# A four-layer graph network on one core: weight factors made one from another, tied to the norm steps of z, in a new order

## The chip, the cores and the metric

The kernel runs on one core of a Trainium2 chip. A core has TensorE (PE) for matmuls, VectorE (DVE), ScalarE (ACT) and GpSimd (POOL) for element-wise work, and SyncE (SP), which here only issues DMAs. Each engine takes its own instructions in the order in which the program lists them and waits for semaphores of the others. The metric is the device time of one execution in microseconds (us). The kernel before took 2358.99 us in the median of three runs (2358.26 to 2367.0).

## The reference

128 graphs of 64 nodes with 512 features each go through four residual layers. Every layer takes `h = max(layernorm(x), 0)` and adds its result to `x`. All is float32.

```
layer 0:  x += hyperconv(norm(relu(hyperconv(h, W1, b1))), W2, b2) + h   # 512 -> 1024 -> 512
layer 1:  A = exp(lrelu(tanh(s_i + s_j))) * adj;  s = (h w) a
          x += (normalised A) h w
layer 2:  weight = adj * exp(query key^T), normalised;  x += weight value
layer 3:  transition = normalised(adj * exp(lrelu(s_j + s_i)))
          H = sum over k = 0..2 of (transition^k h) Wk[k] + bk[k];  x += relu(H)
```

`Wk` is 3 x 512 x 512. The rows of layer 3's bias `bk` add up to one row that is added to every token's `H` before the relu.

## The kernel before

**Tiling.** Two graphs fill the 128 partitions; four such tiles (512 tokens) are a group, and there are 16 groups. Layers 0 and 1 run over all groups first, group after group; their result goes to DRAM (`xmid`) and comes back for layers 2 and 3, which again run over all groups. Two tiles are multiplied by a weight matrix at a time, with Strassen-like schemes of seven block products in place of eight (`strassen`, `seven`, `chained`).

**Layer 0 and 1 of one group.** `part("m")` makes the graph's matrix M from the adjacency (matmul at L777). For each pair of tiles ("h0"/"h1") the norm of x and the left multiplication by M (L579) come first, then seven products with W1 ("p0"/"p1", L678, 512 wide), whose outcome is `z` (L698, L805). Then come z's norm steps ("z0"/"z1"): statistics on DVE (L549, L550), reciprocal root and offset on POOL (L551, L552, L557), scaling on ACT (L817), and a transposition through ACT (L588), a DMA on SP (L589) and ACT again (L590) into `rT`. Seven products with W2 follow ("q0"/"q1", L678, 256 wide), and one with M ("y0"/"y1", L830). Layer 1 ("s", "t0", "e0", "t1", "e1") makes its softmax with a row sent through DRAM and back (`across`, L716 and L720) into the matrix `bd` (L859), then left-multiplies (L579) and runs seven products with w (L678, 256 wide).

**Layer 3.** Its three weight matrices are used in a scheme of 7 x 7 block products of 128 x 128 (L1107, `product`). The weights that it needs are fixed combinations of blocks of `Wk`: seven factors f for each k. `setup_w3` makes one of these 21 pieces: it loads blocks of `Wk[k]` (L521, 256 KB), subtracts them on POOL (`minus`, L525), derives four more tiles on POOL (`factors`, L529 to L531) and stores seven tiles to DRAM (`fac`, four stores at L535). Layer 3 reads them back for each group (L1099, three buffers). In layer 3, `snapshot` (L1116, ACT) copies the running sum of products out of PSUM, `plus` (L1122, DVE) adds another sum to it, and `emit` adds the bias (L1130) and combines tiles (L1131 to L1134), all on POOL, then adds the relu to x on DVE (L1138) and stores the result (L1142).

**Who sets the order.** The program first writes all operations down as a graph (`Graph.op`) with an engine, a cost, a latency and a priority. `Graph.run` then walks through time with these costs and picks on every engine the ready operation with the lowest priority value; the resulting list is emitted. Priorities grow with the group (PERIOD1, PERIOD2), with the work done within a layer (STRETCH), and are shifted by one constant per part (AT). So a changed constant, cost or dependency changes the order of all later instructions, on all engines. Where the walk sees PE idle for over 1 us and a free PSUM bank, `fill` puts in matmuls of ones (L1174) that nobody reads, for three quarters of that time.

**Where the pieces stand.** The pieces of layer 3's weights are written down after group g's layers, with the priority of group g + 1, two in each of the groups 0 to 10; their first load depends on the first tile of group g having been sent to `xmid`.

Of the kernel before, what the change touches and what calls it, by code (L numbers as in the profile page):

```python
# [14 lines left out]
P = 128  # L15
# [153 lines left out]
def tile_adj_preln_d4(  # L169
# [105 lines left out]
    def quad(b):  # L275
# [4 lines left out]

    STRETCH, PERIOD1, PERIOD2 = (2.11, 6.43, 50.7454, 3.1018), 79.8, 149.671
    AT = {
        "x0": -1800.77, "apart": 162.27, "w1": -1056.46, "b1": -1251.68, "w2": 289.41, "w": 187.29, "c1": -506.79,
        "l0": -1396.61, "c2": -766.47, "l1": 284.95, "c": 412.65, "g0": -1390.19, "g1": -1497.17, "g2": -452.82,
        "g3": -792.81, "g": -606.23, "bq": 154.13, "l3": 115.58, "wg": -1172.65, "wp": 197.31, "beg0": -229.22,
        "beg1": -36.07, "end00": 423.2, "end01": 45.77, "end11": 664.32, "new2": 124.83, "new3": -530.75, "end2":
        -7.16, "end3": 48.79, "load1": -431.08, "load2": 1027.47, "m": 12.29, "h0": 9.53, "p0": 10.98, "z0": -29.14,
        "q0": 15.48, "y0": -518.61, "h1": -26.33, "p1": -22.59, "z1": -30.25, "q1": 4.48, "y1": -2.76, "s": -33.08,
        "t0": -25.67, "e0": -522.9, "t1": -42.32, "e1": -53.88, "hT": 483.54, "sh": -254.95, "lq": 629.92, "pt":
        495.66, "v": 131.94, "pv": 641.64, "s3": 571.4, "tt": 605.01, "a0": 651.96, "b0": -437.14, "a1": 681.39,  # L290
        "ws": 401.1, "load3": 250.29, "bk": 902.76,
    }
# [219 lines left out]

    def setup_w3(f, k, when):


        sub, turn = nc.gpsimd.tensor_sub, ["wpturn"]
        src = lambda i, j: Wk3[k].rearrange("(c p) o -> p c o", p=P)[:, 2 * i:2 * i + 2, j * 2 * P:(j + 1) * 2 * P]

        def load(i, j, when=()):
            b = Buf("wp")  # L520
            dma(256, lambda: nc.sync.dma_start(b.t.rearrange("p (q n) k -> p q (n k)", q=2), src(i, j)), when, [b, *turn])  # L521
            return b

        def minus(y, x_, out):
            pool(1.3, lambda: sub(out.t, y.t, x_.t), [y, x_], [out])  # L525

        def factors(F):
            R = Buf("wp")
            pool(0.8, lambda: sub(R.t[:, 1:3], F.t[:, 1::2], F.t[:, 0:2]), [F], [R, *turn])  # L529
            pool(0.53, lambda: sub(R.t[:, 0], F.t[:, 3], R.t[:, 1]), [F, R], [R])  # L530
            pool(0.53, lambda: sub(R.t[:, 3], F.t[:, 2], R.t[:, 0]), [F, R], [R])  # L531
            to = lambda n: fac[f][n].rearrange("p (r k c) -> p r k c", k=3, c=P)[:, :, k, :]
            for n, d, b, v in ((0, slice(0, 2), F, slice(0, 3, 2)), (0, slice(2, 4), R, slice(0, 2)),
                               (1, slice(1, 2), F, slice(3, 4)), (1, slice(0, 3, 2), R, slice(2, 4))):
                dma(128, lambda n=n, d=d, b=b, v=v: nc.sync.dma_start(to(n)[:, d], b.t[:, v]), [b], [("fac", f, n, k, d.start)])  # L535

        terms = (((0, 0),), ((1, 0),), ((1, 1),), ((0, 0), (0, 1), (1, 1), (1, 0)), ((0, 0), (0, 1)),
                 ((0, 0), (0, 1), (1, 1)), ((0, 1), (1, 1)))[f]
        F = load(*terms[0], when)
        for at in terms[1:]:  # L540
            Y = load(*at)
            minus(Y, F, F)
        factors(F)
# [166 lines left out]
    def across(col, r, lat=2.0):  # L710

        b = Buf("rw")
        d = dram.tile([P, T], F32, name=f"row{len(rows)}")
        key = ("row", len(rows))
        rows.append(d)
        dma(4, lambda: nc.sync.dma_start(d, col()), r, [key], lat=lat)  # L716

        def back():
            for s in HALVES:
                nc.sync.dma_start(b.t[s].rearrange("p c t -> p (c t)"), d[s].rearrange("c t -> (c t)").partition_broadcast(C))  # L720
        dma(128, back, [key], [b], 1.2, lat + 0.8 if lat > 2 else 2.0)
        return b
# [35 lines left out]
    def layer0(g):  # L758
# [29 lines left out]
        for t0 in (0, 2):  # L788
# [22 lines left out]
            for i in range(2):  # L811
                z, rT = zs[i], rTs[i]
                mv, rs = norm_stats(lambda k, z=z: z.t[:, k * D:(k + 1) * D], 2, [(z, 0), (z, 1)])
                nm = offset(mv, rs)
                for j in range(2):
                    half = lambda z=z, j=j: z.t[:, j * D:(j + 1) * D]
                    act(0.72, lambda half=half, rs=rs, nm=nm: nc.scalar.activation(half(), half(), AF.Identity, bias=nm.t, scale=rs.t), [(z, j), rs, nm], [(z, j)])  # L817
                    transposed(half, [(z, j)], Buf("tmp"), half, [(z, j)], lambda rT=rT, j=j: rT.t[:, j * KD:(j + 1) * KD, :], [(rT, j)])
                    step(0.1)
# [175 lines left out]
    def layer3(g):  # L995
# [116 lines left out]
        def snapshot(chain):  # L1112
# [4 lines left out]
            return Z  # L1117

        def plus(Z, chain):
            for n, p in enumerate(banks[chain]):  # L1120
# [3 lines left out]
        def emit(i, j, Z):  # L1124


            z = lambda a, b, s=1: Z.t[:, a:b:s]
            add = nc.gpsimd.tensor_add
            cast = lambda n: z(n, n + 1).to_broadcast([P, 2, P])
            pool(0.84, lambda: add(z(0, 4, 3), z(0, 4, 3), bk3_b.t[:, 2 * j * P:2 * (j + 1) * P].rearrange("p (a b) -> p a b", a=2)), [(Z, 0), bk3_b], [(Z, 0)])  # L1130
            pool(0.92, lambda: add(z(1, 3), z(1, 3), cast(0)), [(Z, 0)], [(Z, 0)])  # L1131
            pool(0.92, lambda: add(z(0, 8, 7), z(3, 5), cast(2)), [(Z, 0), (Z, 1)], [(Z, 0), (Z, 1)])
            pool(0.64, lambda: add(z(4, 5), z(7, 8), z(3, 4)), [(Z, 0), (Z, 1)], [(Z, 0), (Z, 1)])
            pool(0.92, lambda: add(z(2, 4), z(5, 7), z(0, 8, 7)), [(Z, 0), (Z, 1)], [(Z, 0), (Z, 1)])  # L1134
            cols = slice(2 * j * P, 2 * (j + 1) * P)
# [9 lines left out]
        product(1, A00, "X", True)  # L1145
        s0 = snapshot("X")
        minus(A11, S2, A00[0], [k[-1] for k in A00[1]])
        product(2, A01, "Y", True)
        plus(s0, "Y")
        emit(0, 0, s0)  # L1150
        product(6, S2, "X", False)
        s1 = snapshot("X")
        minus(A01, S2, A01[0], [k[-1] for k in A01[1]])
        product(5, S1, "X", False)
        s2 = snapshot("X")
        product(3, A01, "X", False)
        s3 = snapshot("X")
        emit(0, 1, s3)
        product(7, A00, "Y", True)
# [35 lines left out]
    for g in range(NG):  # L1195
# [4 lines left out]
        for i, layer in ((0, layer0), (1, layer1)):  # L1200
# [7 lines left out]
            layer(g)  # L1208
        G.prio = (g + 1.0) * PERIOD1
        part("wp")  # L1210
        for i in range(2 * g, min(2 * g + 2, 21)):
            setup_w3(i // 3, i % 3, [("xmid", g, 0)])
    G.prio = NG * PERIOD1
# [9 lines left out]
    for k in range(1, 3):  # L1223
        b = Buf("h")
        dma(256, lambda b=b, k=k: nc.sync.dma_start(b.t, bk3[k].partition_broadcast(P)), [], [b])
        pool(1.3, lambda b=b: nc.gpsimd.tensor_add(bk3_b.t, bk3_b.t, b.t), [b, bk3_b], [bk3_b])
# [69 lines left out]
```

## Time and profile before

| | |
|---|---|
| median of three runs | 2358.99 us |
| profiled execution | 2356.54 us, span 2354.7 us |
| PE busy | 2299.0 us in 14296 matmuls |
| DVE, ACT, POOL busy | 1932.6, 1385.8, 1209.2 us |
| mean DMA rate | 153 GB/s; over 200 GB/s from 1295 us on |
| layers 0 and 1 | from the start to about 1240 us |
| layers 2 and 3 | from about 1210 us to the end |
| pieces of layer 3's weights | loads from 167.7 to 901.6 us |

The span runs from the first to the last instruction. The times of a row in the groups of instructions are the sum over all instructions of that form and the mean of one; the idle time that follows is that of the engine just before them, with the instruction that ended it. A PE instruction's end is modelled, so a wait of PE that is shorter than about 0.16 us does not show as idle time.

### The profile page before, as it was taken

How to read it: one execution, taken by the hardware profiler on the slowest of the kernel's cores; microseconds unless marked ns; L12 is line 12 of the kernel's file. 1: busy time of each engine (PE TensorE's matmuls, PEld its weight loads, DVE VectorE, ACT ScalarE, POOL GpSimd, SP SyncE). 2: the span in 40 equal slices, each digit the busy share in tenths (PEclk: the TensorE clock that was granted, in tenths of full speed). 3: DMA queues.
4: the chain of work that ended last, by engine and by line, in shares of the span. 5: the costliest groups of instructions: out<-in, count | busy, mean ns of one | idle time of the engine just before them, and what ended most of it. 6: DMA issues, size and time to landing. Idle time of an engine off the chain costs nothing.

```text
span 2354.7 us, 39854 instructions
## 1 busy us (share of the span) xinstructions
PE 2299.0 (98%) x14296; PEld 1868.4 (79%) x14296; DVE 1932.6 (82%) x4000; ACT 1385.8 (59%) x1986; POOL 1209.2 (51%) x1777
## 2 busy tenths in 40 slices
PE   9999999999999999999999999999999999999997
PEld 4676667766677666777688899899999999999997
DVE  7968788788888788887867888888888888888886
ACT  4566465765556656576556666565566656566642
POOL 6334565456755566544433555455554545555533
PEclk9999999999999999999999999999999999999999
DMA  8333333333434333232335878777887777787767
GB/s 264 77 75 79 76 92 91 90 71 110 106 94 106 80 93 91 72 81 59 81 77 160 230 217 228 219 210 214 250 228 217 225 214 216 214 249 230 206 199 224
DMA packets 408374, 359.85 MB, mean 153 GB/s; under 512 B 291184, under 2 KB 326768, under 8 KB 408176
## 3 DMA queue, kind: packets, MB, share of 16 engines
q1 hardware_dynamic: 408176, 357.30, 56.1%
q8 instruction: 113, 1.85, 0.3%
q14 instruction: 85, 0.70, 0.1%
HBM read 245.77 MB, written 44.33 MB: 123 GB/s over the span
## 4 chain that ended last, share of the span: by engine, by line
PE 68%; DVE 12%; DMA 10%; ACT 4%; POOL 3%; issue 2%; SPq 1%; POOLq 0%; DVEq 0%; ACTq 0%
PE ps L678 28%; PE ps L1107 18%; PE ps L916 13%; PE ps L579 4%; DMA w2m_wm_a_wf<-fac 3%; PE ps L1053 2%; DMA z_hT<-tmp_mB_xi 2%; DVE rT_vu_tt L1022 2%; PE ps L985 2%; PE ps L830 1%; DMA rw<-row 1%; DVE st L549 1%; DMA h<-o 1%; POOL rs L552 1%; ACT tmp_mB_xi L588 1%
## 5 line engine op out<-in xcount | busy, mean ns | idle before, releaser
L570 ACT ACTIVATE h<-x,nm,rs 128x512 f32<-128x512 f32 x384 | 306.0, 814 | 153.5 <-POOL nm L557 133.3
L551 POOL TENSOR_SCALAR rs<-mv 128x1 f32<-128x1 f32 x320 | 117.1, 366 | 364.5 <-DVE mv L550 345.1
L1107 PE MATMUL ps<-w2m_wm_a_wf 128*128 128x128 f32 x2304 | 298.7, 276 | 2.3 <-DMA w2m_wm_a_wf<-fac 2.2
L1107 PEld LDWEIGHTS ps<-w2m_wm_a_wf 128*128 128x128 f32 x2304 | 280.9, 192 | 8.3 <-DMA w2m_wm_a_wf<-fac 1.9
L678 PE MATMUL ps<-w2m_wm_a_wf,s_s_zz 128*128 128x256 f32 x1152 | 277.3, 380 | 6.3 <-DVE s_s_zz L670 4.0
L1107 PE MATMUL ps<-w2m_wm_a_wf,tmp_mB_xi 128*128 128x128 f32 x2016 | 262.6, 275 | 0.9 <-DMA w2m_wm_a_wf<-fac 0.7
L678 PEld LDWEIGHTS ps<-w2m_wm_a_wf,s_s_zz 128*128 128x128 f32 x1152 | 215.4, 190 | 58.8 <-issue 18.4
L1107 PEld LDWEIGHTS ps<-w2m_wm_a_wf,tmp_mB_xi 128*128 128x128 f32 x2016 | 243.9, 192 | 3.6 <-issue 1.2
L678 PE MATMUL ps<-w2m_wm_a_wf,rT_vu_tt 128*128 128x256 f32 x1024 | 238.8, 380 | 5.7 <-ACT rT_vu_tt L590 5.7
L678 PE MATMUL ps<-wa_mem,mT_sx 128*128 128x512 f32 x512 | 236.1, 593 | 0.7 <-ACT mT_sx L581 0.6
L678 PEld LDWEIGHTS ps<-w2m_wm_a_wf,rT_vu_tt 128*128 128x128 f32 x1024 | 192.2, 190 | 49.7 <-issue 13.9
L552 POOL TENSOR_TENSOR rs<-rs,mhalf 128x1 f32<-128x1 f32 x320 | 209.9, 656 | 26.4
L805 ACT ACTIVATE z_hT<-z_hT 128x512 f32<-128x512 f32 x128 | 80.1, 628 | 208.9 <-DVE z_hT L698 205.4
L549 DVE BATCH_NORM_STATS2 st<-x 128x6 f32<-128x512 f32 x256 | 173.4, 682 | 26.7 <-DMA x<-xm 20.1
L678 PE MATMUL ps<-wa_mem,s_s_zz 128*128 128x512 f32 x384 | 180.1, 595 | 4.5 <-DVE s_s_zz L670 4.1
L678 PEld LDWEIGHTS ps<-wa_mem,mT_sx 128*128 128x128 f32 x512 | 96.3, 190 | 107.1 <-issue 98.8
L706 POOL TENSOR_TENSOR u<-u,row_sh 128x256 f32<-128x256 f32 x96 | 76.2, 804 | 173.0 <-DVE u L648 144.3
L557 POOL TENSOR_SCALAR nm<-mv,rs 128x1 f32<-128x1 f32 x320 | 146.0, 456 | 31.3
L590 ACT COPY rT_vu_tt<-z_hT 128x1024 uint16<-128x1024 uint16 x128 | 146.7, 1158 | 22.9 <-DMA z_hT<-tmp_mB_xi 22.4
L579 PEld LDWEIGHTS ps<-bd,h 128*128 128x128 f32 x1024 | 131.0, 194 | 29.8 <-DVE bd L859 11.8
L968 POOL TENSOR_TENSOR u<-u,wp_bv_bk 128x512 f32<-128x512 f32 x48 | 67.9, 1414 | 153.8 <-ACT u L621 153.8
L588 ACT COPY o<-h 128x1024 uint16<-128x1024 uint16 x128 | 132.2, 1043 | 23.8 <-DVE h L1044 21.3
(191 smaller groups left out, 5116.7 us busy)
## 6 DMA issues: line engine op xcount, KB each, us to landing
w2m_wm_a_wf<-fac SPq DMA_DIRECT2D x112, 768.0 KB, 5.6
w2m_wm_a_wf<-fac SPq DMA_DIRECT2D x112, 576.0 KB, 4.9
x<-xm SPq DMA_DIRECT2D x128, 256.0 KB, 3.9
x<-in_x_dram SPq DMA_DIRECT2D x64, 256.0 KB, 2.8
xm<-x SPq DMA_DIRECT2D x64, 256.0 KB, 2.1
out_dram<-x SPq DMA_DIRECT2D x64, 256.0 KB, 2.8
wp_bv_bk<-in_Wk_dram SPq DMA_DIRECT2D x42, 256.0 KB, 3.0
adj<-in_adj_dram SPq DMA_DIRECT2D x32, 256.0 KB, 4.2
```

Source lines behind the costliest of these rows:

```text
L549: dve(0.69, lambda i=i: nc.vector.bn_stats(st.t[:, i, :], src(i)), [r[i]], [(st, i)])
L551: pool(0.32, lambda: nc.gpsimd.tensor_scalar_add(rs.t, mv.t[:, 1:2], EPS), [mv], [rs])
L552: pool(0.65, lambda: nc.gpsimd.tensor_tensor(rs.t, rs.t, mhalf, ALU.pow), [rs], [rs])
L557: pool(0.47, lambda: nc.gpsimd.tensor_scalar(nm.t, mv.t[:, 0:1], rs.t, -1.0, op0=ALU.mult, op1=ALU.mult), [mv, rs], [nm])
L570: act(0.82, lambda: nc.scalar.activation(h.t, xx.t, AF.Relu, bias=nm.t, scale=rs.t), [xx, nm, rs], [h])
L579: nc.tensor.matmul(quad(p)[:, c, :], h.t[:, c * P:(c + 1) * P], rhs(), start=True, stop=True)
L588: act(1.05, lambda: nc.scalar.copy(u16(planes.t).rearrange("p (q c) -> p q c", q=2), u16(src()).rearrange("p (c q) -> p q c", q=2)), ksrc, ...
L590: act(1.16, lambda: nc.scalar.copy(u16(dst()).rearrange("p c (k q) -> p c k q", q=2), u16(back()).rearrange("p (q c r) -> p c r q", q=2, c ...
L678: nc.tensor.matmul(p.t[:, :n], lhs()[:, c, :], rhs(c), start=first and c == 0, stop=c == kc - 1, skip_group_check=True)
L805: act(0.63, lambda: nc.scalar.activation(z.t[:, cols], z.t[:, cols], AF.Relu), [(z, j)], [(z, j)])
L916: nc.tensor.matmul(pair(p.t)[:, o, :], a, b, start=first and o == 0 and c == 0, stop=c == 1, skip_group_check=True)
L1107: nc.tensor.matmul(inner(p, q)[:, r, :], at()[:, k, :], w_.t[:, r, k, :], start=first and r == 0 and k == 0, stop=k == 2, skip_group_check ...
```

## The change

Five things are changed.

1. `setup_w3`: the factors of each k are now made in the sequence 0, 4, 5, 3, 1, 2, 6, k after k. Factor 0's tile stays in its buffer (`chain3`), and the next three are each made from the last by one subtraction. A k needs 8 loads and 4 subtractions, where it was 14 and 7.
2. The pieces' place: none stands in group 0, two in each of the groups 1 to 10 and one in group 11, with the priority of group g. The loads depend on the end of z's offset (L557) of an earlier half, the POOL work on the end of z's offset of a half of group g.
3. The bias of layer 3 is added by `bias` right after each snapshot, no longer inside `emit`.
4. The last `emit` of the program, that of block (1, 0) of group 15, runs its four adds on DVE.
5. All of STRETCH, PERIOD1, PERIOD2 and AT have new values; `across` is written down with a latency longer by 1.3 us (write) and 0.7 us (read) where layer 3 calls it; `minus` with 1.35 us in place of 1.3; the second and third load of `bk` wait for the first.

```diff
-    STRETCH, PERIOD1, PERIOD2 = (2.11, 6.43, 50.7454, 3.1018), 79.8, 149.671
+    STRETCH, PERIOD1, PERIOD2 = (1.9884, 2.1221, 50.9861, 3.7462), 79.959, 161.557
     AT = {
-        "x0": -1800.77, "apart": 162.27, "w1": -1056.46, "b1": -1251.68, "w2": 289.41, "w": 187.29, "c1": -506.79,
+        "x0": -2165.99, "apart": 359.07, "w1": 560.57, "b1": -128.79, "w2": 2266.0, "w": 629.08, "c1": 83.74, "l0":
...
-    def setup_w3(f, k, when):
+    chain3 = {}
+
+    def setup_w3(n, when, at):
+        k, n = n // 7, n % 7
+        f, blocks = ((0, ((0, 0),)), (4, ((0, 1),)), (5, ((1, 1),)), (3, ((1, 0),)), (1, ((1, 0),)), (2, ((1, 1),)), (6, ((0, 1), (1, 1))))[n]
...
-            pool(1.3, lambda: sub(out.t, y.t, x_.t), [y, x_], [out])
+            pool(1.35, lambda: sub(out.t, y.t, x_.t), [y, x_, *at], [out])
...
-            pool(0.8, lambda: sub(R.t[:, 1:3], F.t[:, 1::2], F.t[:, 0:2]), [F], [R, *turn])
+            pool(0.8, lambda: sub(R.t[:, 1:3], F.t[:, 1::2], F.t[:, 0:2]), [F, *at], [R, *turn])
...
-        terms = (((0, 0),), ((1, 0),), ((1, 1),), ((0, 0), (0, 1), (1, 1), (1, 0)), ((0, 0), (0, 1)),
-                 ((0, 0), (0, 1), (1, 1)), ((0, 1), (1, 1)))[f]
-        F = load(*terms[0], when)
-        for at in terms[1:]:
-            Y = load(*at)
+        got = [load(*b) for b in blocks]
+        F = chain3[k] if 0 < n < 4 else got.pop(0)
+        if n == 0:
+            chain3[k] = F
+        for Y in got:
             minus(Y, F, F)
         factors(F)
...
-        dma(4, lambda: nc.sync.dma_start(d, col()), r, [key], lat=lat)
+        dma(4, lambda: nc.sync.dma_start(d, col()), r, [key], lat=lat + 1.3 if lat > 2 else 2.0)
...
-        dma(128, back, [key], [b], 1.2, lat + 0.8 if lat > 2 else 2.0)
+        dma(128, back, [key], [b], 1.2, lat + 1.5 if lat > 2 else 2.0)
...
                 nm = offset(mv, rs)
+                G.last_write["z", g, k] = G.ops[-1]
...
+        def bias(j, Z):
+            add = nc.gpsimd.tensor_add
+            pool(0.84, lambda: add(Z.t[:, 0:4:3], Z.t[:, 0:4:3], bk3_b.t[:, 2 * j * P:2 * (j + 1) * P].rearrange("p (a b) -> p a b", a=2)), [(Z, 0), bk3_b], [(Z, 0)])
...
-            add = nc.gpsimd.tensor_add
+            last = g == NG - 1 and (i, j) == (1, 0)
+            add, on = (nc.vector.tensor_add, lambda c, *a: dve(c * 0.55, *a)) if last else (nc.gpsimd.tensor_add, pool)
             cast = lambda n: z(n, n + 1).to_broadcast([P, 2, P])
-            pool(0.84, lambda: add(z(0, 4, 3), z(0, 4, 3), bk3_b.t[:, 2 * j * P:2 * (j + 1) * P].rearrange("p (a b) -> p a b", a=2)), [(Z, 0), bk3_b], [(Z, 0)])
-            pool(0.92, lambda: add(z(1, 3), z(1, 3), cast(0)), [(Z, 0)], [(Z, 0)])
...
+            on(0.92, lambda: add(z(1, 3), z(1, 3), cast(0)), [(Z, 0)], [(Z, 0)])
...
         s0 = snapshot("X")
+        bias(0, s0)
...
         s1 = snapshot("X")
+        bias(0, s1)
...
         s2 = snapshot("X")
+        bias(1, s2)
...
-        G.prio = (g + 1.0) * PERIOD1
+        G.prio = g * PERIOD1
         part("wp")
-        for i in range(2 * g, min(2 * g + 2, 21)):
-            setup_w3(i // 3, i % 3, [("xmid", g, 0)])
+        if g:
+            for k in range(2):
+                if 2 * g - 2 + k < 21:
+                    setup_w3(2 * g - 2 + k, [("z", g - 1 + k, 1 - k)], [("z", g, k)])
...
-        dma(256, lambda b=b, k=k: nc.sync.dma_start(b.t, bk3[k].partition_broadcast(P)), [], [b])
+        dma(256, lambda b=b, k=k: nc.sync.dma_start(b.t, bk3[k].partition_broadcast(P)), [bk3_b], [b])
```

## The prediction, made before the changed kernel was run

> **What bounds the kernel now.** First the page's busy times, and PE's row in its 40 slices:
>
> ```profile
> PE 2299.0 (98%) x14296; PEld 1868.4 (79%) x14296; DVE 1932.6 (82%) x4000; ACT 1385.8 (59%) x1986; POOL 1209.2 (51%) x1777
> ...
> PE   9999999999999999999999999999999999999997
> ```
>
> PE sets the time. It idles 55.7 of 2354.7 us, so nothing outside its instructions can gain more than that. Where it idles is asked of the windows (columns: window, its length, busy us of PE, weight loads, DVE, ACT and POOL with instruction counts, PE clock, DMA share, GB/s). I cut them at 152 (the first groups are in), at 943 (the pieces' last work), at 1150 to 1296 (layers change) and at the last groups:
>
> ```profile
> 0.00:152.00 152.00, 141.73 (x549) 86.05 (x549) 121.32 (x246) 84.86 (x119) 64.33 (x100) 0.99 0.52 143
> 152.00:943.00 791.00, 776.48 (x3350) 552.57 (x3351) 648.12 (x1365) 473.24 (x661) 453.76 (x692) 1.00 0.37 91
> 943.00:1150.00 207.00, 206.55 (x901) 150.63 (x900) 163.00 (x358) 125.31 (x177) 101.00 (x161) 1.00 0.28 67
> 1150.00:1296.00 146.00, 143.09 (x849) 118.59 (x849) 107.31 (x240) 93.29 (x133) 47.25 (x89) 1.00 0.46 118
> 1296.00:2290.00 994.00, 978.74 (x8170) 910.34 (x8167) 850.35 (x1721) 592.16 (x875) 516.27 (x703) 1.00 0.79 222
> ```
>
> The reader is to compare the second line with the third. Both are the same layers 0 and 1. With pieces PE idles 14.5 us in 791 (1.84%), without them 0.45 in 207 (0.22%). At the lower rate the 791 us would idle 1.7, so 12.8 us is the most that a better place for the pieces can give. What PE waits for in 152 to 943 (columns: total us, times, longest):
>
> ```profile
> POOL wp_bv_bk L525 <- DMA wp_bv_bk<-in_Wk_dram: 28.7, 8, 8.8
> POOL wp_bv_bk L529 <- DMA wp_bv_bk<-in_Wk_dram: 14.5, 6, 3.5
> PE ps L579 <- DVE bd L859: 6.1, 6, 1.9
> ```
>
> POOL runs in order, and stands up to 8.8 us at a subtraction (L525) whose block has not landed; z's offset and layer 1's work on POOL are queued behind it, and DVE's softmax matrix (`bd`) then reaches PE late. PE's other waits there are 3.8 us for DVE's products' inputs (L670), 3.7 for `rT` from ACT (longest 1.4) and 1.4 for x. In layers 2 and 3 PE waits longest for layer 3's own loads:
>
> ```profile
> PE ps L1107 <- DMA w2m_wm_a_wf<-fac: 7.8, 9, 1.7
> ```
>
> **The Trainium skill.** "Perfetto Trace Analysis", section "Tensor Engine Instruction (MATMUL, LD_WEIGHTS)": the other engines' wait queues feed strictly ordered execution queues, and a matmul's end is estimated. The 8.8 us stand of POOL agrees with the order; for the ends I use start-to-start pitches (0.429 us for a 512-wide matmul of layer 0's W1, 0.216 for 256 wide, 0.112 for 128 wide). "SBUF — State Buffer", section "🔬 SBUF: two separate sides": DVE and GpSimd share a port pair as an exclusive lock. L525 takes 1.26 to 1.77 us for one shape, which agrees but does not prove it. "GPSIMD Engine Reference", section "4.1 Engine selection": a two-input add is about twice as slow on GpSimd; here 0.72 us for 128x256 (L1132) against 0.42 on DVE (L872).
>
> **The change part by part**, summed against the profiled execution's 2356.5 us (the median is 2.45 above it).
>
> *Tail, −0.9.* The end in the timeline:
>
> ```profile
> 2347.57 0.56 DVE L1122 TENSOR_TENSOR s_s_zz<-ps,s_s_zz 128x384 f32<-128x384 f32 x1
> 2348.27 0.72 POOL L1132 TENSOR_TENSOR s_s_zz<-s_s_zz 128x256 f32<-128x256 f32 x1 [0.24 <-DVE s_s_zz L1122]
> 2349.07 0.46 POOL L1133 TENSOR_TENSOR s_s_zz<-s_s_zz 128x128 f32<-128x128 f32 x1
> 2349.60 0.72 POOL L1134 TENSOR_TENSOR s_s_zz<-s_s_zz 128x256 f32<-128x256 f32 x1
> 2350.36 0.76 DVE L1138 SCALAR_TENSOR_TENSOR x<-s_s_zz,x 128x256 f32<-128x256 f32 x2 [2.23 <-POOL s_s_zz L1134]
> ```
>
> From L1122's end (2348.13) to L1138's start POOL needs 2.23. On DVE the three adds cost 0.42 + 0.28 (halved tile, between 0.21 and 0.42) + 0.42 = 1.12, with some 0.1 between them. The gain is 1.0; the preceding block's relu instructions stand ahead of L1131 on DVE, so I take 0.9, range 0 to 1.05. The bias (L1130, 64 of 947 ns) goes to before the last product; the same instruction runs, it only leaves the tail, where it was already over at 2347.2.
>
> *Pieces in 152 to 943, −9.8.* 18 loads of 256 KB and 9 subtractions fewer: 9 × 1.37 = 12.3 us of POOL and 18 × about 0.4 of SP's issue, none of it on PE's path by itself. What counts is the waits behind them. A piece's loads now start a half earlier than its work, so POOL no longer stands at L525 (28.7) or L529 (14.5). Ties to z's offset put the 2.9 us of piece work after the offset that z needs. And the order gives more cover: counting the matmuls listed between producer and user, z's norm to its first W2 product had 6 products of 1.72 + 0.86 + 1.72 + 0.9 = about 13.8 us ahead of it, and has one M product (0.86) and one left multiplication (0.89) more, 15.5. The softmax matrix had 23.0 to 25.6 and gets 27.3. Waits of at most 1.4 (`rT`) and 1.9 (`bd`) against 1.75 and about 2.6 more cover are gone: 3.7 + 6.1. The 3.8 of L670 and the 1.4 for x I leave. Bounds: −12.8 as above, or 0 if these waits had another source: two of the longest go back to a late softmax row and a late transposition, no piece.
>
> *New tight places, +1.* In the changed order a copy of layer 1's second half on ACT (L646, 0.37 us) must end within one product of 0.86 us, where it had at least 1.7. ACT waits for PE there now, not PE for ACT. Range 0 to +5.
>
> *Head, −1.* Five fill matmuls more (32 to 37 before the layers settle) at 0.223 cost 1.1; PE's longest wait there, 2.9 us for the first W2 product, sits in the old order. Range −3.5 to +3.
>
> *Change of layers, +4.8.* The fills (columns: start, duration, then what ran, how often; two instructions make one matmul):
>
> ```profile
> 1195.21 3.73 PE L1174 MATMUL ps<-ones 128*128 128x128 f32 x32
> 1200.07 1.99 PE L678 MATMUL ps<-w2m_wm_a_wf,rT_vu_tt 128*128 128x256 f32 x8 [1.13 <-ACT rT_vu_tt L590]
> ```
>
> 32 instructions are 16 fill matmuls at 0.223. PE still waits 1.13 after them: the fills cover a real wait. Between the layers there were 37 such matmuls, and will be 55: 18 × 0.223 = 4.0, with 0.8 of wait left after them (they fill three quarters of the time that the order foresees as idle). Fills cannot be skipped, so this is paid even if the data come earlier. Other side: fewer idle holes elsewhere in that stretch return up to 4.8, range 0 to +6.
>
> *Layers 2 and 3, 0.* The loads from `fac` stand in nearly the same sequence on SP, with the same 5.99 us of products between the buffer's release and its use; only the place of layer 2's products among them differs. Range −2 to +4. Longer latencies of `across` and the wait among the `bk` loads issue nothing new; they only shift the order, which is already counted; hidden by 100s of us of cover before layer 3.
>
> Sum: −0.9 − 9.8 + 1 − 1 + 4.8 + 0 = −5.9, so 2350.6 for a profiled execution, and 2353.0 on the median's scale.
>
> **Rivals.** *A, the pieces were all of it.* Idle time falls to the rate of the stretch without pieces: −12.8, head −3.5, tail −0.9, change of layers 0: 2359.0 − 17.2 = 2341.8. For it: the third window line. Against it: 18 more fills that must run, and the two waits above that come from no piece.
>
> *B, ACT becomes the bound of layer 1 (slower).* The new order is the same in twelve groups, so one tight place is paid twelve times. If an activation of z (about 1.05 us with its neighbour's 0.59 copy) stands ahead of L646, PE is late by 1.5 us per group: +18 in place of the +1 and of part of the gain, 2359.0 + 12 = 2371. It decides once ACT is over 0.3 us late at that copy, twice per group. Against it: ACT is 60% busy and waits for PE at L646 28 times, 19.9 us in the whole span.
>
> *C, nothing arrives.* The waits have another source, the row through DRAM (42.3 us of DVE's waits, which PE mostly does not see) or the transposition (3.1 us, as long with pieces' DMAs beside it as without); gains and fills cancel: 2359 + 4.8 − 0.9 − 1 = 2362.
>
> *D, a new wait in place of the old one.* The stores of a piece wait for POOL on SP's queue, and z's transposition (L589) is issued behind them. A piece takes 2.9 us of POOL after the offset, z's scaling and first transposition about 1.9 on ACT; SP then is 1.0 late, within the 1.75 of added cover. It costs from 0.75 us more on, then about 1 per piece: 21 in place of nothing, 2353 + 21 = 2374.
>
> **How the numbers follow.** A measurement of this kernel can tell about 0.5%, 11.8 us. The forecast as summed, with its own range of 2346 to 2360, has 0.45; C 0.10; A 0.25; B and D together 0.20. A lies below 2347.2 and most of B and D above 2370.8. Part of the forecast's low end adds 0.03 to faster, and the ends of C and of a bad change of layers 0.02 to slower: faster 0.28, within 0.5% 0.50, slower 0.22. Leaving out a tenth on each side gives 2338 to 2370.
>
> **What would show it.** POOL's waits at L525 and L529 for DMA under 10 us in place of 43.2; PE's wait at L579 for `bd` under 2 us; no `rT` wait over 0.5 in groups 2 to 11; idle PE in 152 to 943 near 5 us. 226 fill instructions in place of 180, and PE idle at the change of layers about as before. The tail from last matmul to end 6.3 us in place of 7.2. B shows as PE's wait at L678 for ACT's L646 or DVE's L670, alike in each group; D as SP standing at L535 ahead of L589. The prediction is wrong if a wait repeats in every group, or if layers 2 and 3 move by over 4 us though their order hardly changes.

## The result and the profile after

The changed kernel took 2351.77 us in the median of 14 runs (2345.95 to 2356.56), the kernel before beside it 2358.7 (2356.51 to 2367.0). The ratio is 0.9965, with a 95% interval of 0.9954 to 0.9976: about 8 us, or 0.35%, which is less than 0.5%. It was measured once more beside some of the experiments below: 0.9968 (0.9956 to 0.9979). The profiled execution has a span of 2345.6 us, where that of before had 2354.7.

The page of the changed kernel, busy times and PE's row in its 40 slices:

```profile
PE 2301.3 (98%) x14342; PEld 1876.8 (80%) x14342; DVE 1936.0 (83%) x4004; ACT 1386.6 (59%) x1986; POOL 1201.9 (51%) x1764
...
PE   9999999999999999999999999999999999999998
```

PE has 46 instructions more, the 23 matmuls of ones that were foreseen, and idles 44.3 us in place of 55.7. The windows of the changed kernel (window, length, busy us of PE, weight loads, DVE, ACT, POOL, clock, DMA share, GB/s):

```profile
0.00:152.00 152.00, 141.62 (x546) 85.49 (x547) 124.38 (x252) 87.59 (x122) 73.42 (x113) 0.99 0.51 149
152.00:943.00 791.00, 787.53 (x3423) 566.52 (x3422) 637.23 (x1380) 478.82 (x671) 445.24 (x675) 1.00 0.35 85
943.00:1150.00 207.00, 205.55 (x891) 147.93 (x890) 162.64 (x351) 129.92 (x178) 103.87 (x166) 1.00 0.30 71
1150.00:1296.00 146.00, 142.05 (x908) 122.91 (x907) 108.70 (x237) 86.89 (x128) 51.34 (x90) 1.00 0.44 116
1296.00:2290.00 994.00, 978.71 (x8146) 909.72 (x8145) 866.26 (x1720) 590.08 (x869) 509.85 (x697) 1.00 0.81 222
```

In 152 to 943, PE's idle time has gone from 14.5 to 3.5 us; in each of the other windows it has moved by about 1 us at most. All that PE waited for in that window (total us, times, longest):

```profile
PE ps L583 <- DVE bd L864: 3.8, 5, 2.1
PE ps L835 <- DVE y_qT L712: 1.0, 1, 1.0
PE ps L583 <- ACT h L574: 0.6, 1, 0.6
```

Lines are four to thirteen higher in the changed kernel (L579 is L583 now, L859 is L864, L670 is L674, L1174 is L1187). The waits for `rT`, for the products' sums on DVE (L670) and for x are gone, and `bd` is down from 6.1 to 3.8, of which 2.1 stand at 151.4 us, before a group is steady. POOL's waits for pieces, 43.2 us in 14 stands before, are gone too: its only wait for that buffer and a DMA is now one for the bias rows, L1241.

A window that is fixed in time holds other work in each kernel. A table at equal work is better. Its marks are the starts of the last product with M of layer 0 (L830) in groups 2 and 12, of layer 2's last product (L985) in group 2 and of layer 3's last product in group 15, found in each trace by counting PE's instructions in the program's order. The second column is safe, since both orders repeat from group to group there, and PE runs the same 3120 instructions in it besides fills; the columns beside it carry a constant, since the marks stand a little differently among the other work in each order.

| profiled execution (us) | start to layer 0, group 2 | to group 12 | to layer 2, group 2 | to the last product | to the end |
|---|---|---|---|---|---|
| before | 267.4 | 737.9 | 378.8 | 962.6 | 8.0 |
| changed | 268.4 | 723.9 | 382.1 | 964.4 | 6.9 |
| changed, measured again | 266.1 | 722.8 | 380.9 | 966.1 | 6.9 |

The gain is in ten steady groups of layers 0 and 1, 14 to 15 us, or 1.4 per group. The change of layers gives back 2 to 3, the tail gives 1.1. Layers 2 and 3 took 962.6 to 968.4 us in all traces of this study with nearly the same order, so their 2 to 3.5 us here are scatter. The second column scatters less: in six traces that have the changed order there (these two and the four of the fill matmuls below) it lies between 722.8 and 724.0.

Not all of the 14 us is idle time of PE. In the second column, first before, then changed:

```profile
267.39:1005.32 737.93, 724.76 (x3128) 515.19 (x3126) 608.45 (x1274) 446.30 (x624) 424.13 (x640) 1.00 0.36 90
268.36:992.23 723.87, 720.54 (x3122) 516.54 (x3121) 586.10 (x1271) 444.04 (x621) 409.26 (x621) 1.00 0.36 85
```

Idle time falls from 13.2 to 3.3 us, by 9.8. The other 4.2 us is in PE's busy time: 0.7 for three fill matmuls that only the old order has there (3 × 0.223), the rest in the same matmuls. The clock is no rival for the gain: neither trace has a stretch at half clock between these marks.

The tail in the timeline of the changed kernel, on DVE now:

```profile
2339.54 0.56 DVE L1131 TENSOR_TENSOR s_s_zz<-ps,s_s_zz 128x384 f32<-128x384 f32 x1 [0.32 <-PE ps L1112]
2340.14 0.42 DVE L1141 TENSOR_TENSOR s_s_zz<-s_s_zz 128x256 f32<-128x256 f32 x1
2340.60 0.29 DVE L1142 TENSOR_TENSOR s_s_zz<-s_s_zz 128x128 f32<-128x128 f32 x1
2340.92 0.43 DVE L1143 TENSOR_TENSOR s_s_zz<-s_s_zz 128x256 f32<-128x256 f32 x1
2341.38 0.76 DVE L1147 SCALAR_TENSOR_TENSOR x<-s_s_zz,x 128x256 f32<-128x256 f32 x2
```

From the end of the last sum (2340.10) to L1147 it is 1.28 us, where POOL needed 2.23: 0.95 gained. Each add costs what was read from the rows of before (0.42, 0.29, 0.43), and the bias is out of the way.

### The profile page after: what moved, and what is told of

Same layout as the page of the kernel before. It is cut to its first block, busy times and chain, and to the rows that moved or that the text cites. A ratio compares the mean times of both kernels' runs of the same rounds, so it can differ in the third digit from the quotient of the medians.

```text
span 2345.6 us, 39929 instructions
## 1 busy us (share of the span) xinstructions
PE 2301.3 (98%) x14342; PEld 1876.8 (80%) x14342; DVE 1936.0 (83%) x4004; ACT 1386.6 (59%) x1986; POOL 1201.9 (51%) x1764
## 4 chain that ended last, share of the span: by engine, by line
PE 75%; DMA 9%; DVE 9%; ACT 3%; POOL 2%; issue 2%; SPq 0%; DVEq 0%; POOLq 0%; ACTq 0%
PE ps L682 35%; PE ps L921 13%; PE ps L1112 13%; PE ps L583 5%; DMA w2m_wm_a_wf<-fac 4%; PE ps L1058 2%; PE ps L990 2%; DVE o L382 2%; PE ps L835 2%; DMA x<-xm 2%; PE ps L952 1%; DVE st L553 1%; DMA wa_q<-o 1%; PE ps L468 1%; DMA rw<-row 1%
## 5 line engine op out<-in xcount | busy, mean ns | idle before, releaser
L555 POOL TENSOR_SCALAR rs<-mv 128x1 f32<-128x1 f32 x320 | 102.5, 320 | 349.0 <-DVE mv L554 329.6
L561 POOL TENSOR_SCALAR nm<-mv,rs 128x1 f32<-128x1 f32 x320 | 160.9, 504 | 30.4
L583 PEld LDWEIGHTS ps<-bd,h 128*128 128x128 f32 x1024 | 128.7, 194 | 35.0 <-issue 17.1
L822 ACT ACTIVATE z_hT<-z_hT,nm,rs 128x512 f32<-128x512 f32 x128 | 103.8, 813 | 73.3 <-POOL nm L561 73.3
```

The lines of the kernel that those rows point to most:

```text
L555: pool(0.32, lambda: nc.gpsimd.tensor_scalar_add(rs.t, mv.t[:, 1:2], EPS), [mv], [rs])
L561: pool(0.47, lambda: nc.gpsimd.tensor_scalar(nm.t, mv.t[:, 0:1], rs.t, -1.0, op0=ALU.mult, op1=ALU.mult), [mv, rs], [nm])
L583: nc.tensor.matmul(quad(p)[:, c, :], h.t[:, c * P:(c + 1) * P], rhs(), start=True, stop=True)
```

## The experiments

Two explanations of the 14 us have to be told apart. In the *wait theory*, POOL's stands at late blocks of the pieces made PE late, and the pieces' new form ended that. In the *order theory*, the old order of layers 0 and 1 had too little cover whatever the pieces did, and the new constants ended that. Where an edit says that the order is kept, every instruction that stays is issued in the same sequence on its engine.

**Both kernels without the pieces' work, order kept.** The loads and POOL instructions of 20 of the 21 pieces are left out, so layer 3's weights are not made. In both kernels alike, here as in the one before:

```diff
-            dma(256, lambda: nc.sync.dma_start(b.t.rearrange(...), src(i, j)), when, [b, *turn])
+            dma(256, (lambda: nc.sync.dma_start(b.t.rearrange(...), src(i, j))) if first else (lambda: None), when, [b, *turn])
...
-            pool(0.8, lambda: sub(R.t[:, 1:3], F.t[:, 1::2], F.t[:, 0:2]), [F], [R, *turn])
+            pool(0.8, (lambda: None) if not first else lambda: sub(R.t[:, 1:3], F.t[:, 1::2], F.t[:, 0:2]), [F], [R, *turn])
```

> The kernel before in its own order, with the loads and all POOL work of 20 of the 21 pieces left out (their stores stay, so layer 3's weights are wrong). Wait theory (POOL standing at pieces' late blocks makes PE late): PE's idle time in 152 to 943 falls from 14.5 to about 3 us, the kernel is 8 us faster (5 to 12.8). Order theory (too little cover in the old order, whatever the pieces do): bd and rT waits stay, 0 to 3 us faster.

> The changed kernel in its own order, with the loads and all POOL work of 20 of the 21 pieces left out (stores stay, layer 3's weights are wrong). Wait theory: the change has already taken the pieces off PE's path, so at most 1 us faster than the changed kernel, and level with the kernel before without its pieces but for the tail and the change of layers. Order theory: also about 0 to 1 us faster, but then 5 us or more ahead of the kernel before without its pieces in layers 0 and 1. If pieces still cost something here: 2 to 4 us faster.

Measured: 0.9968 (0.9957 to 0.9980) for the kernel before without pieces and 0.9955 (0.9943 to 0.9967) for the changed one, both against the whole kernel before. So all of the pieces together cost the old order 0.32%, 7.5 us, and the new order 0.10 to 0.13% (0.9965 or 0.9968 against 0.9955), 2 to 3 us, which is at the edge of what the intervals tell. At equal work, from group 2 to 12: 729.2 and 718.5 us. In that stretch the pieces cost 8.7 us in the old order (737.9 − 729.2) and 4.3 to 5.4 in the new; without these pieces the new order is still 10.7 us ahead. In the new order four waits of PE for `bd`, of 0.2 to 0.7 us, go with the pieces (441, 585, 658 and 731 us); they are 1.7 of those 4.3 to 5.4. What PE waits for in the old order without pieces, in 152 to 943:

```profile
PE ps L678 <- DVE s_s_zz L670: 3.4, 9, 0.5
PE ps L579 <- DVE bd L859: 2.8, 4, 1.6
PE ps L678 <- DVE x L831: 1.4, 2, 0.7
PE ps L678 <- DVE x L872: 0.8, 3, 0.3
PE ps L678 <- ACT rT_vu_tt L590: 0.4, 1, 0.4
```

Of the old waits for `rT` (3.7) and `bd` (6.1), 3.3 and 3.3 us were the pieces' doing. The others stand there unchanged. They are small and come back from group to group; first the kernel before, then the same without pieces, both in PE's timeline:

```profile
417.75 3.70 PE L678 MATMUL ps<-wa_mem,s_s_zz 128*128 128x512 f32 x8 [0.45 <-DVE s_s_zz L670]
452.57 1.99 PE L678 MATMUL ps<-w2m_wm_a_wf,s_s_zz 128*128 128x256 f32 x8 [0.69 <-DVE x L831]
```

```profile
414.54 3.70 PE L678 MATMUL ps<-wa_mem,s_s_zz 128*128 128x512 f32 x8 [0.38 <-DVE s_s_zz L670]
449.38 1.99 PE L678 MATMUL ps<-w2m_wm_a_wf,s_s_zz 128*128 128x256 f32 x8 [0.70 <-DVE x L831]
```

So both theories hold a part, and the order's part is the larger one in this stretch: 3 to 4 us by the pieces, 10.7 by the order. What the old order had ahead of such a wait for DVE's sum (L670) is read from the timeline of the kernel before without pieces, ACT, DVE and PE:

```profile
485.48 0.81 ACT L570 ACTIVATE h<-x,nm,rs 128x512 f32<-128x512 f32 x1
486.20 0.56 ACT L581 COPY mT_sx<-ps 128x512 f32<-128x512 f32 x1
486.70 0.66 DVE L382 SCALAR_TENSOR_TENSOR o<-h,wa_q 128x512 f32<-128x512 f32 x1
487.28 0.42 DVE L670 TENSOR_TENSOR s_s_zz<-mT_sx 128x256 f32<-128x256 f32 x1
487.76 3.70 PE L678 MATMUL ps<-wa_mem,s_s_zz 128*128 128x512 f32 x8 [0.38 <-DVE s_s_zz L670]
```

The copy `mT` (L581) feeds DVE's sum (L670) and that the next seven W1 products. ACT takes a normalisation of x (L570, 0.81 us) ahead of the copy. But the copy is there at 486.76, and the sum starts 0.5 us later: DVE first takes L382, which reads such a normalised x (`h`). In the new order neither stands ahead, and the sum starts when the copy ends:

```profile
340.40 0.58 ACT L585 COPY mT_sx<-ps 128x512 f32<-128x512 f32 x1
341.01 0.43 DVE L674 TENSOR_TENSOR s_s_zz<-mT_sx 128x256 f32<-128x256 f32 x1 [0.29 <-ACT mT_sx L585]
...
343.15 0.81 ACT L574 ACTIVATE h<-x,nm,rs 128x512 f32<-128x512 f32 x1
```

This is a reading of timelines; no run moved these instructions alone, and it explains one kind of the repeated waits, not all of the 10.7 us.

**The pieces ahead of z's norm, order otherwise kept.** Is the tie to the end of z's norm steps worth anything?

```diff
                 mv, rs = norm_stats(lambda k, z=z: z.t[:, k * D:(k + 1) * D], 2, [(z, 0), (z, 1)])
+                if i == 1:
+                    o = G.ops[-2]
+                    o.fn = lambda o_fn=o.fn, key=(g, k): ([q() for q in early.get(key, [])], o_fn())
                 nm = offset(mv, rs)
...
+        def pool(cost, fn, r, w):
+            early.setdefault(at[0][1:], []).append(fn)
+            return G.op("POOL", cost, lambda: None, r, w)
```

> The changed kernel with each piece's POOL work issued ahead of the reciprocal root and offset of the half's second tile, in place of behind them; all else in the same order. If the tie to the end of z's norm steps matters: rT of the second tile is later by 2.9 us (4.3 with a subtraction), which is beyond the 1.75 us of added cover: about 1.2 us per piece, 24 us slower than the changed kernel (10 to 40). If the cover alone carries it: within 3 us of the changed kernel.

Measured: 1.0058 (1.0044 to 1.0071), so 21 us slower than the changed kernel (1.0058 − 0.9968 = 0.0090). From group 2 to 12 it takes 741.0 us in place of 723.9; an estimated 5.1 of these 17 us (3 × 1.7) are three stretches at half clock, which the last section looks at. But PE does not wait where the prediction had counted the cover, at the W2 products for `rT`. The longest and the `rT` wait of this kernel in 152 to 943 (the two others there are 0.8 and 0.5; its lines are four higher than the changed kernel's; L678 here is the sum on DVE):

```profile
PE ps L686 <- DVE s_s_zz L678: 18.5, 9, 2.8
PE ps L686 <- ACT rT_vu_tt L598: 0.5, 1, 0.5
```

It is the copy `mT` again, now on ACT's side: POOL late, z's four ACT instructions late (3.6 us together), the copy behind them late, DVE's sum late, and then the other half's W1 products. The sizes agreed with the forecast by luck.

**A smaller delay at the same place.** Two reciprocal roots of one element per partition ahead of the second tile's norm steps, in the 21 halves that have a piece:

```diff
+                if i == 1 and 2 <= 2 * g + k < 23:
+                    o = G.ops[-2]
+                    late = lambda: [nc.gpsimd.tensor_tensor(late_t, ones[:, :1], mhalf, ALU.pow) for _ in range(2)]
+                    o.fn = lambda o_fn=o.fn: (late(), o_fn())
```

> The changed kernel with two more reciprocal roots of one element per partition (about 0.67 us each, 1.33 us together) on POOL ahead of the offset of the half's second tile, in the 21 halves that have a piece. Cover theory: 1.33 us is within the added cover of 1.75 us, so within 3 us of the changed kernel, where 2.9 us or more cost 22 us; it also shows that 28 us more of POOL's work cost nothing by themselves. If every delay of z is paid: 21 x 1.33 = 28 us slower; if POOL's amount of work counts (the 12.3 us that the change saves): 12 us or more slower.

Measured: 0.9999 (0.9987 to 1.0012), 7 us slower than the changed kernel, where under 3 was expected of the cover. From group 2 to 12 it takes 728.6 us, 4.7 more. PE's timeline and ACT's and DVE's beside it show the place:

```profile
338.27 1.17 POOL L821 TENSOR_TENSOR late<-ones,mhalf 128x1 f32<-128x1 f32 x2
...
343.45 1.04 ACT L593 COPY tmp_mB_xi<-z_hT 128x1024 uint16<-128x1024 uint16 x1
344.40 0.58 ACT L586 COPY mT_sx<-ps 128x512 f32<-128x512 f32 x1
345.01 0.42 DVE L675 TENSOR_TENSOR s_s_zz<-mT_sx 128x256 f32<-128x256 f32 x1 [1.43 <-ACT mT_sx L586]
345.49 1.13 PE L683 MATMUL ps<-wa_mem,s_s_zz 128*128 128x512 f32 x2 [0.46 <-DVE s_s_zz L675]
```

1.17 us of delay give 0.46 us of wait. The new order's slack at this copy is thus about 0.7 us and not 1.75, and `rT` is not what is late first. The run with the pieces ahead says the same: a piece without a subtraction holds POOL for 1.89 us there (563.33 to 565.22) and gives a wait of 1.10, one with a subtraction 3.23 (338.43 to 341.66) and 2.45. Each time all but 0.7 to 0.8 us arrives at PE. The wait comes back once per group, with 0.45 to 0.65 us from 345 us on. That only so much of POOL's work counts as passes this slack also answers whether POOL's amount matters: 42 × 0.561 = 23.6 us more of it cost 7 us here, 4.8 of them in waits for DVE's sums (L675).

**The pieces and the constants, each alone.** The order is worked out anew in both. First the kernel before with the new `setup_w3`, its place and its ties:

```diff
-        for i in range(2 * g, min(2 * g + 2, 21)):
-            setup_w3(i // 3, i % 3, [("xmid", g, 0)])
+        if g:
+            for k in range(2):
+                if 2 * g - 2 + k < 21:
+                    setup_w3(2 * g - 2 + k, [("z", g - 1 + k, 1 - k)], [("z", g, k)])
```

> The kernel before with the change's setup_w3, its place and its ties alone (parts 1 and 2); constants, tail, bias and across as before, so the order is worked out anew from the old constants. If the pieces' rewrite by itself takes the waits away: PE's idle time in 152 to 943 falls from 14.5 to about 8 us, as without pieces, ratio to the kernel before 0.997 to 0.998. If it helps only with the new constants: 0.999 to 1.002. If the old constants place the new pieces badly: over 1.002.

Measured: 0.9983 (0.9973 to 0.9994), 4 us faster than before, between two of the expected cases. From group 2 to 12: 735.8 us, 2.1 less than before; POOL does not stand at a piece any more, but PE's small waits for DVE's sums stay:

```profile
PE ps L682 <- DVE s_s_zz L674: 4.8, 11, 0.5
PE ps L583 <- DVE bd L864: 2.5, 4, 0.9
PE ps L682 <- ACT rT_vu_tt L594: 1.8, 3, 0.8
```

(From the waits of 200 to 1000 us.) Then the changed kernel with the old `setup_w3` in its old place:

```diff
-        G.prio = g * PERIOD1
+        G.prio = (g + 1.0) * PERIOD1
         part("wp")
...
+        for i in range(2 * g, min(2 * g + 2, 21)):
+            setup_w3(i // 3, i % 3, [("xmid", g, 0)])
```

> The changed kernel with the old setup_w3 and the old place of the pieces (parts 1 and 2 undone); constants, tail, bias and across of the changed kernel, order worked out anew. If the order's cover is a gain of its own and the old pieces cost their 7.5 us on top of it: ratio 0.998 to 0.999. If the new constants' cover also hides the old pieces: 0.996 to 0.997. If the new constants need the new pieces: over 1.001, with fill matmuls and a repeated wait in layers 0 and 1.

Measured: 1.0067 (1.0053 to 1.0081), 16 us slower than before and 23 slower than the changed kernel. The list now has fill matmuls in steady groups, pairs like these in PE's timeline:

```profile
792.17 1.28 PE L1183 MATMUL ps<-ones 128*128 128x128 f32 x10
...
795.78 2.39 PE L1183 MATMUL ps<-ones 128*128 128x128 f32 x20
```

From group 2 to 12 this kernel takes 742.4 us, 18.6 more than the changed one. Of these, 13.9 are in PE's busy time, with 58 fill matmuls there (12.9 us at 0.223) where the changed kernel has none, and 4.7 in its idle time. So the parts cannot be added up. The new constants pay only with the new pieces. The new pieces alone bring half of the gain in time, but only 2.1 of 14 us in layers 0 and 1; the rest of their 4 us lies in layers 2 and 3 (958.4 us to the last product), whose order moved as well.

**Late loads, order otherwise kept.** The 12 loads whose blocks are subtracted are issued when their subtraction comes up:

```diff
-            pool(1.35, lambda: sub(out.t, y.t, x_.t), [y, x_, *at], [out])
+            pool(1.35, lambda: (late.pop(0)(), sub(out.t, y.t, x_.t)), [y, x_, *at], [out])
...
-        got = [load(*b) for b in blocks]
+        late = []
+        got = [load(*b, *([late.append] if 0 < n < 4 or m else [])) for m, b in enumerate(blocks)]
```

> The changed kernel with the 12 loads whose blocks are subtracted issued on SP only when their subtraction comes up on POOL, as late as before; all else in the same order. Wait theory: POOL stands about 2.5 to 3 us at 12 subtractions (some 30 us in all), and what is queued behind them is late for PE: 3 to 8 us slower than the changed kernel. If only work ahead of z's offset hurts, and what is behind the pieces has slack: within 2 us of it.

Measured: 0.9978 (0.9966 to 0.9989), beside 0.9968 for the changed kernel: not told apart. The edit did not bring about what it was made for. SP is far enough ahead of POOL that the blocks were there in most cases:

```profile
POOL wp_bv_bk L529 <- DMA wp_bv_bk<-in_Wk_dram: 4.8, 4, 1.9
```

4.8 us of standing and not 30. Even so, it took 726.0 us from group 2 to 12, outside the 722.8 to 724.0 of the six traces, with three waits of PE for DVE's sums (1.4 us) that the changed kernel does not have; it is one trace. It leaves open what long stands of POOL behind z's norm would cost in the new order.

**The fill matmuls.** The prediction took each matmul of ones for paid. Without those at the change of layers, with as many as before, and with a third more everywhere:

```diff
-        for _ in range(int(gap * FILL / (0.224 if filled else 0.448))):
+        for _ in range(0 if 5 <= len(filled) < 10 else int(gap * FILL / (0.224 if filled else 0.448))):
```

> The changed kernel without the 55 matmuls of ones between 1140 and 1270 us. If they run where PE would not have had to wait, as the prediction priced them: 4 us faster (up to 12.3 if none covers a wait). If they only fill real waits: 0. If PE's clock falls without them: 1 to 5 us slower, with a lower granted clock in 1140 to 1290.

```diff
+        for _ in range({5: 5, 6: 3, 7: 5, 8: 16, 9: 8}.get(len(filled), int(gap * FILL / (0.224 if filled else 0.448)))):
```

> The changed kernel with 37 matmuls of ones at the change of layers (5, 3, 5, 16 and 8) in place of 55, as many as the kernel before has. Priced as in the prediction, 18 x 0.223: 4 us faster than the changed kernel. If they fill real waits and hold the clock, as the run without any of them says: 0 to 3 us slower.

> The changed kernel with 37 matmuls of ones at the change of layers once more; the first time its runs fell in two groups, near 2348 and near 2356 us, and a third more fill matmuls cost nothing. If the 18 fill matmuls matter: again 0.999 to 1.001 and two groups. If the groups are none of the fills' doing: 0.996 to 0.998, as the changed kernel beside the kernel before.

```diff
+        for _ in range(int(gap * FILL * 4 / 3 / (0.224 if filled else 0.448))):
```

> The changed kernel with every run of fill matmuls a third longer (the whole of the foreseen gap in place of three quarters, some 37 matmuls more). If fills hold PE's clock through waits that are real: 0 to 4 us faster. If each is paid, at 0.223 us: 8 us slower. If they fit into waits and the clock does not fall there anyway: within 2 us.

Measured: 1.0003 (0.9992 to 1.0014) with none, 1.0000 (0.9987 to 1.0013) and 0.9996 (0.9985 to 1.0007) with 37, 0.9971 (0.9959 to 0.9983) with a third more. On balance none of them is paid at 0.223 us: a third more cost nothing that can be told, and taking them away makes the kernel 7 to 9 us slower. Without fills, PE waits longer at the same places, for instance here at the change of layers:

```profile
1254.75 5.66 PE L921 MATMUL ps<-z_hT,wa_mem 128*128 128x256 f32 x16 [5.74 <-ACT z_hT L594]
```

and the clock falls there, to half (the columns are those of the windows above; the clock is the third number from the end):

```profile
1252.00:1255.00 3.00, 0.25 (x1) 0.25 (x2) 2.86 (x10) 1.94 (x3) 1.91 (x5) 0.50 0.69 137
1255.00:1258.00 3.00, 3.00 (x8) 2.37 (x9) 1.82 (x6) 2.60 (x3) 1.83 (x2) 0.50 0.00 0
```

In all, the records show 13.7 us of half clock at 1146, 1252 and 1450 us, where the first profile of the changed kernel has none between 155 us and its last product; the profiled execution is 4.8 us longer. The mean granted clock of each run is on record too, and settles it for the run without fills: 0.9944 in the mean of its 14 runs, where the two measurements of the changed kernel have 0.9976 and 0.9971. Over 2350 us that is an estimated 13 us of lost clock in place of 5.5 and 7, so 6 to 8 of the 8 to 9 us. The fills' worth there is that PE's clock does not fall.

With 37 fills it is settled in part only. The two profiled executions are level with the changed kernel up to the mark in layer 2 (382.1 and 380.4 in the third column). But the 14 runs of the second lie between 2347.6 and 2357.3 us and those of the changed kernel on the same chip between 2344.6 and 2350.6, and no trace is of one of the longer runs. Their mean clocks, 0.9964 and 0.9965, account for 1.5 to 3 of the 7 to 8 us; what makes the rest stays open. With a third more, 42 matmuls, the clock was 0.9986, an estimated 3.5 us less lost than in the changed kernel beside it: these fills may cost a little and give it back.

**The changed kernel once more**, as the control for all of these:

> The changed kernel once more, beside the kernel before on the chip of this call. The 22 us of the early pieces, the 8 us of the two roots and the 8 us of the 18 fill matmuls were all taken against a ratio of 0.9965 from elsewhere. If that holds here: 0.9954 to 0.9976. If this chip gives the change less: 0.998 to 1.000, and those three costs shrink by as much.

Measured: 0.9968 (0.9956 to 0.9979), as the first time. It ran beside the late loads and the third more fills. The other experiments ran where only the kernel before stood beside them, so their distance to the changed kernel goes through the two ratios. Nothing that computes the whole result came out faster than it; the version with a third more fills is the same within the interval.

## Why the prediction was right, and where its steps failed

The time, 2353.0 forecast against 2351.77, and the case, faster by under 0.5%, came true. That the sum came so near is in part luck: it said −5.9, and the medians moved by −6.9, but the two profiled executions by −9.1 and −11.9. Layers 0 and 1 gave 4 to 5 us more than forecast, and the change of layers took about 2 less; scatter in layers 2 and 3 and the spread of the runs hid that.

- *Tail, −0.9*: 0.95 between the last sum and the relu, as worked out.
- *Pieces in 152 to 943, −9.8 (and +1 for tight places)*: 14 to 15 us at equal work. What failed is the sentence "The 3.8 of L670 and the 1.4 for x I leave": those were the old order's own repeated waits, present with and without pieces, and the new order ended them. The `rT` and `bd` waits that it did count were about two thirds the pieces' doing (6.6 of 9.8). `rT`'s 3.7 went; `bd` kept 3.8 (1.6 when measured again) of 6.1, where under 2 was the sign. The bound of 12.8, taken from idle time, was exceeded because idle time is only 9.8 of the 14; 4.2 are in PE's busy time, 0.7 of them in fills. What made the same matmuls take 3.5 us less there is open; waits shorter than about 0.16 us, which do not show as idle time, are one candidate.
- *The cover*: "Waits ... against 1.75 and about 2.6 more cover are gone" named the wrong constraint. The counted cover between z's norm and the W2 products is not what limits: delays of 1.2 to 3.2 us on POOL brought no new repeated `rT` wait. ACT's queue limits: z's four instructions stand ahead of the copy `mT`, with 0.7 us of slack. The count looked at what PE does between producer and user, and not at what else the producer's engine has queued in front of another user's input.
- *The order of the pieces behind z's offset*: shown. Ahead of it they cost 21 us, an estimated 5 to 7 of them by a lower clock (0.9948 in the mean of the runs).
- *Head, −1*: +1.0 and −1.3 in two executions; not told from nothing.
- *Change of layers, +4.8*: 2 to 3 by the marks. Its reason, 18 fill matmuls at 0.223, is refuted: 37 of them in place of 55 leave the marks where they are and the median higher. They run inside waits that are there anyway, and keep the clock up in them. What the 2 to 3 us are instead was not found.
- *Layers 2 and 3, 0*: within the scatter of traces.
- *Rival A* (all of the pieces' cost goes, fills free): even with no piece's work at all the changed kernel is only at 0.9955, 2348 on the scale of the 2358.7, and not at 2341.8. *Rival B*: ACT's L646 was never late for PE. Its idea, an ACT queue as the bound of a repeated place, was right in kind, but the place is the copy `mT`, and in the new order it costs only once POOL is more than 0.7 us late. *Rival D*: half of it happened. SP stood at the pieces' stores for POOL:

```profile
SPq L539 <- POOL wp_bv_bk L529: 113.9, 9, 19.9
```

but PE had no wait for `rT` in steady groups (one of 0.3 us when measured again); z's transpositions behind these stores were not late enough to matter. *Rival C* fell with the first table.

The step on queues that the Trainium skill's page "Perfetto Trace Analysis", section "Tensor Engine Instruction (MATMUL, LD_WEIGHTS)", was cited for, strictly ordered execution queues, carried more than was made of it: it is why a late scaling on ACT delays a copy that it has nothing to do with.

## What to carry to other kernels

Waits of a few tenths of a microsecond that come back from group to group can add up to as much as the long ones (7 us of idle time in ten groups without pieces, 6 more with them), and they are told from the effects of a suspected cost by leaving that cost out in the unchanged order: what stays is the order's. When cover is counted, count it for everything that is queued behind the delayed instruction on its engine, not only for its own user. A filler matmul is not priced by its length; ask whether the wait that it sits in would be there without it, and what the clock does in that wait. And compare at equal work: a bound taken from idle time leaves out what hides in busy time.

## What was not expected of the hardware

The granted clock falls to half in stretches of 3.413 us (five of 6.827 in the fourteen traces; only those behind the last product have other lengths), and these begin at distances that are whole multiples of 3.413 us: in the run with the pieces first, 14, 43, 42, 109 and 44 of them between six such stretches. Each costs PE at most 1.7 us, half of its 3.413. Here are two waits of one length in that run, with eight instructions behind each:

```profile
347.62 5.22 PE L686 MATMUL ps<-wa_mem,s_s_zz 128*128 128x512 f32 x8 [2.45 <-DVE s_s_zz L678]
423.34 3.70 PE L686 MATMUL ps<-wa_mem,s_s_zz 128*128 128x512 f32 x8 [2.44 <-DVE s_s_zz L678]
```

Half clock begins at 347.3 beside the first, and none follows the second. They differ in where they lie on the grid of 3.413 us. The grid period that ends at 347.3 holds 2.13 us of the first wait; the second is split at 422.4, into 1.5 and 0.95. This holds throughout: with PE's idle time of the profile added up in each period of the grid (counted in each trace from one of its half-clock stretches), from 75 us on in all fourteen traces, each of the 15 periods with 1.84 us or more is followed by half clock, and none of the 9274 others, which have 1.73 at most. In the first 75 us idle time does not separate them so.

The Trainium skill's page "TensorE: Matmul & The Clock Gate", section "What's actually happening", tells of a free-running window of 3413 ns over which activity is judged, and the distances and this hit and miss agree with it. Its table there has half clock after one idle window of about 3.4 us; here about 1.8 us of idle time within one was enough, and the measurement decides. So the same wait can cost its length in one run and up to 1.7 us more in the next. This is a source of the spread of some 10 us between runs of one kernel and not the whole of it: in the first measurement of the changed kernel the two runs with a mean clock of 0.996 took 2355.0 and 2356.6 us, the two with 0.999 took 2346.8 and 2352.2.
